# A constant matrix product in light steps, an allowance for transfers, an earlier input request and a dropped carry copy, in a scan kernel fused with an MLP

## The chip, the core and the metric

The kernel runs on one core of one Trainium2 chip. A core has five engines that each execute their own instruction queue in order: PE (TensorE, matrix products), DVE (VectorE), ACT (ScalarE), POOL (GpSimd) and SP (SyncE, which here only issues DMAs). All values are fp32. The metric is device time in microseconds of one execution, and the time before is a median of three runs.

## The reference

The input `x` is 8 images of 64 x 64 pixels with 96 channels. Two layers follow each other, each with a residual. The first normalises groups of channels, projects to 2 x 192 channels (`xc` and a gate `z`), filters `xc` with a 3 x 3 depthwise convolution and SiLU, and runs a selective scan over the 4096 pixels in four orders (`K = 4`: rows, columns, and both backwards) with 192 channels of 16 states:

```python
def step(h, inp):
    ul, dl, Bl, Cl = inp
    dA = jnp.exp(dl[..., None] * A)
    h = dA * h + (dl * ul)[..., None] * Bl[:, :, None, :]
    y = jnp.einsum('bkdn,bkn->bkd', h, Cl)
    return (h, y)
```

The four results are added, normalised, multiplied by the gate and projected back to 96 channels. The second layer normalises again, doubles the image's size in both directions by a Fourier filter, applies a matrix of 96 x 384, a quadratic polynomial and a matrix of 384 x 96, filters and samples down again, and adds the residual.

## The kernel before

**The scan steps.** One image has 4 orders (`k` = 1, 0, 2, 3) of 4 chunks of 1024 pixels, and each chunk has 24 tiles (`NT`) of 8 channels x 16 states = 128 partitions. That makes 16 chunks and 384 tiles per image, 3072 in all. The main loop makes one step per tile. The work of a tile is spread over the engines:

- `fetch` (L1004): SP issues a DMA that brings `dub`, 8 rows of `dl * u` each repeated over 16 partitions, 6 steps ahead. There are 4 buffers, so the DMA of tile i+6 waits until POOL has used that of tile i+2.
- `product_b` (L1012): POOL multiplies `dub` by B, 3 steps ahead.
- `decay` (L1016): PE spreads `dl` over the states into PSUM tile `pd` (2 products, 2 buffers), one step ahead, and ACT takes the exponential in place.
- `scan` (L1029): DVE runs the recurrence. `product_c` (L1038): DVE multiplies by C in two of three tiles; in the third (`by_pool`) POOL does, a step later. `hold` (L1042): a copy of the last state into column `g` of `carry`, on DVE, or on ACT for the `by_pool` tiles; the next chunk's scan of the same channels starts from it.
- `sums` (L1054): every second step PE adds states up into `py`, and `store` sends it to DRAM every 8 tiles.

Since `pd` has two buffers, `decay` of tile i+1 on PE waits until DVE is done with tile i-1.

**The input of a chunk.** `prepare` (L911) makes what the 24 tiles share: `begin` asks for `u` (two DMAs on SP, one buffer), `project` multiplies it on PE into `px`, and `delta` makes `dl` and `du` in three thirds. The main loop (L1151) asks for the next chunk's `u` in step 20 of 24; `project` stands first among the side work of step 0.

**The side work.** While the scan of image b runs, the rest of image b-1 (`tail`, L604, which normalises and gates the scan's result, then `mlp`, L737) and the start of image b+1 (`front`, L474, with `conv`, `lay` and `gate`) run as generators that a planner, `Side`, advances once per step. A generator yields what its next piece costs, in us per engine. A step gives each engine an allowance (`CAPS`, first number), which can be saved up to the second number; a piece that doesn't fit waits for a later step. Pieces also need one of three PSUM banks (`side.free`). DMAs cost nothing in this account: `load_x` issues one 192 KB transfer per step, `tail.begin` (loads `ye`) four per three steps, `tail.block` four at once (`ty`, `tz`), `lay` one per step. `advance` runs after `hold`, so on PE the side work of step i stands between `decay` of tile i+1 and `sums`, and all of it ahead of `decay` of tile i+2. In the last image `tail` starts within the fourth order, and its `mlp` runs after the last scan.

Of the kernel before, what the change touches and what calls it, by code (L numbers as in the profile page):

```python
# [23 lines left out]
NCH = L // T  # L24
MB = 512
NT = DI // 8
# [11 lines left out]
class Side:  # L38
# [7 lines left out]

    CAPS = dict(pe=(2.2, 2.9), act=(2.3, 3.0), dve=(1.5, 1.5), pool=(1.4, 2.7))

    def __init__(self, pool):
        self.pool = pool
        self.free, self.given = list(range(BANKS)), []
        self.urgent, self.hurried, self.later = [], [], []
        self.queue, self.active = [], []
        self.stores = []
        self.alone = {}
        self.begun = 0
        self.caps, self.left = None, {}

    def bank(self, name):
        n = self.free.pop(0)
# [9 lines left out]
    def emit(self, entry, spare):  # L72

        first = True
        while entry[1] is not None:
            need = dict(entry[1])
            banks, more = need.pop("bank", 0), need.pop("more", False)
            if need.pop("holds", False):
                spare = 0
            if not (first or more) or (banks and len(self.free) - spare < banks):  # L80
                return True
            if self.caps:
                if any(c > self.left[e] for e, c in need.items()):
                    return True
                for e, c in need.items():
                    self.left[e] -= c
            entry[1] = next(entry[0], None)
            first = False
        return False
# [15 lines left out]
    def advance(self, caps, more=1, spare=1, taken=0.0):  # L105

        self.caps = caps
        if caps:
            self.left = {e: min(self.left.get(e, 0.0) + c, most) for e, (c, most) in caps.items()}
            self.left["pe"] -= taken
        self.free += self.given
        self.given = []
        for active, spare_ in ((self.stores, 0), (self.hurried, 0), (self.active, spare)):
            for entry in list(active):
                if not self.emit(entry, spare_):
                    active.remove(entry)  # L120
            for _ in range(2):
                if self.urgent and active is self.hurried:
                    self.start(self.urgent, self.hurried, 0)
        for _ in range(more):
            if not self.queue or not self.start(self.queue, self.active, spare):
                break
# [7 lines left out]
def kernel(ctx: ExitStack, tc: tile.TileContext, a: dict, out: bass.AP):  # L134
    nc = tc.nc
    x = a["x"]
# [17 lines left out]
    ident = load("ident", [128, 128])  # L154
# [43 lines left out]
    sel_b = cp.tile([128, 8, NS, 8], F32, name="sel_b")  # L198
# [18 lines left out]
    with tc.tile_pool(name="ps0", bufs=1, space=PSUM) as ps0, tc.tile_pool(name="setup", bufs=1) as c0p:  # L217
# [55 lines left out]
        for j in (9, 7, 5, 3):  # L273
            c = (1.0 if j % 4 == 1 else -1.0) / math.factorial(j)
# [19 lines left out]
        for quarter in range(2):  # L294
            grid = wave[:, cols[SIDE, quarter]]
            start, stop = quarter == 0, quarter == 1
# [4 lines left out]
                start=start,  # L301
                stop=stop,
                skip_group_check=True,
            )
        for quarter in range(2):
            grid = wave[:, cols[SIDE, quarter]]
            start, stop = quarter == 0, quarter == 1
# [50 lines left out]
    side = Side(pss)  # L358
# [25 lines left out]
    bp = Room()  # L384
# [10 lines left out]
    def load_x(t, b):  # L395

        for w in range(0, 32, 8):
            for wh in range(2):
                w0 = 32 * wh + w
                nc.sync.dma_start(t[64 * wh : 64 * wh + 64, w : w + 8, :], x[b, :, w0 : w0 + 8, :])  # L400
                yield {}


    def pause(n):
# [69 lines left out]
    def front(b):  # L474
# [4 lines left out]
        v, got = {}, {}  # L479
# [10 lines left out]
            z_dram[b] = dr.tile([DI, L], F32, tag="z", name="z")  # L490

        def piece(g):
            yield {}
            t = bp.tile([128, 4, C], F32, tag="x", name="x", bufs=4)
            for wh in range(2):
                w0 = 32 * wh + 4 * g
                nc.sync.dma_start(t[64 * wh : 64 * wh + 64], x[b, :, w0 : w0 + 4, :])
            yield {}
            yield {}
            yield {}  # L500
            return t
# [55 lines left out]
        def lay(n):  # L557

            yield {}
            while not all((b, n, blk) in filtered for blk in range(8)):  # L560
                yield {}
            yield {}
            for h0 in range(0, H, 8):
                h1 = h0 + 8
                if n == 0:
                    src = v["xt"][0][:, h0:h1].rearrange("p h w -> p (h w)")
                    nc.sync.dma_start(u_dram[b][0][0:128, W * h0 : W * h1], src)
                else:
                    u = u_dram[b][0][128:192].rearrange("c (h w) -> c h w", h=H)
                    for p in range(2):  # L570
                        nc.sync.dma_start(u[:, h0:h1, 32 * p : 32 * p + 32], v["xt"][1][64 * p : 64 * p + 64, h0:h1])
                yield {}
            laid.add((b, n))

        def gate(n, g):
# [22 lines left out]
        parts, last = stats_items(piece, lambda: v["pad"], got)  # L598
        start = [bp.open("front"), (1, 1, begin), *parts, last, (4, 4, norm)]
# [4 lines left out]
    def tail(b, keep, pairs=True):  # L604

        v = {}

        def begin():
            yield {}
            keep["x1"] = bp.tile([128, 32, C], F32, tag="x", name="x", bufs=1, depth=0)  # L610
            while (b, "even") not in summed:
                yield {}
            v["ye"] = [bp.tile([C, H, W], F32, tag=f"ye{f}", name=f"ye{f}", bufs=1) for f in range(HF)]
            for h0 in range(0, H, 8):
                for f in range(HF):
                    nc.sync.dma_start(
                        v["ye"][f][:, h0 : h0 + 8].rearrange("p h w -> p (h w)"),
                        y_dram[b][0][f * C : f * C + C, W * h0 : W * h0 + 8 * W],
                    )
                    if f == 1 or h0 % 16:  # L620
                        yield {}
            yield {}
            yield {}

        def block(g):
# [5 lines left out]
            yz = [bp.tile([C, HF, 8, H], F32, tag=tag, name=tag, bufs=n) for tag, n in (("ty", 4), ("tz", 3))]  # L631
            for t, src in zip(yz, (y_dram[b][1], z_dram[b])):
                for f in range(HF):
                    nc.sync.dma_start(
                        t[:, f].rearrange("p w h -> p (w h)"), src[f * C : f * C + C, MB * g : MB * g + MB]
                    )
# [13 lines left out]
            for f in range(HF):  # L650
# [3 lines left out]
                t = two[f][1]  # L654
# [10 lines left out]
            n = two[0][0]  # L665
            t = side.again(n, "pn")
# [23 lines left out]
            halves = (0, 1) if pairs else (g // 4,)  # L690
            g %= 4
            rows = slice(64 * halves[0], 64 * halves[-1] + 64)
            for _ in range(3):
                yield {}
            for i0 in (0, 4):
                yield dict(bank=1, pe=1.7)
                n, t = side.bank("po")
# [3 lines left out]
                for i in range(4):  # L701
                    if i == 2:
                        yield dict(pe=0.87, act=0.5, more=True)
                    for f in range(HF):
                        for wh in halves:
# [4 lines left out]
                                start=False,  # L710
                                stop=(f == 1),
# [6 lines left out]
            if not v["left", g]:  # L718
                keep["done"].add(g)

        def piece(g):
            yield {}
            while g // 2 not in keep["done"]:
                yield {}
            return keep["x1"][:, 4 * g : 4 * g + 4, :]
# [3 lines left out]
        parts, keep["last"] = stats_items(piece, None, keep["got"])  # L729
        blocks += [parts[g] for g in (6, 7, 4, 5, 2, 3, 0, 1)]  # L730
        return (
            [bp.open("residual"), bp.open("tail"), (1, 1, begin), (4, 0, lambda: load_x(keep["x1"], b))]
            + blocks
            + [bp.close()]
        )

# [250 lines left out]
    tiles = []  # L987
    for b in range(images):
        for k in (1, 0, 2, 3):
            order = range(NCH) if k < 2 else range(NCH - 1, -1, -1)  # L990
            for n, c in enumerate(order):
                got = {}
                for i in range(NT):
                    q, n8 = divmod(i, 8)
                    s, j = n8 % 2, n8 // 2
                    tiles.append(
                        dict(b=b, k=k, i0=c * T, first=n == 0, i=i, q=q, s=s, j=j, g=8 * q + 4 * s + j, got=got)
                    )
                    tiles[-1]["by_pool"] = i % 3 == 2
    carry = pp.tile([128, NT], F32, tag="carry", name="carry", bufs=1)  # L1000

# [36 lines left out]
    def product_c(t):  # L1038
        t["hc"] = sp.tile([128, T], F32, tag="hc", name="hc", bufs=4)
        (nc.gpsimd if t["by_pool"] else nc.vector).tensor_tensor(t["hc"], t["h"], t["got"]["cr"], ALU.mult)  # L1040

    def hold(t):  # L1042
        end = T - 1 if t["k"] < 2 else 0
        (nc.scalar.copy if t["by_pool"] else nc.vector.tensor_copy)(  # L1044
            carry[:, t["g"] : t["g"] + 1], t["h"][:, end : end + 1]
        )
# [61 lines left out]
    with tc.manual_schedule():  # L1108
# [4 lines left out]
        n = len(tiles)  # L1113
# [8 lines left out]
        for i in range(n + 4):  # L1122
            t = tiles[i] if i < n else None
            at = i % (NT * NCH * K)
            if t and t["i"] == 0:
                b = t["b"]
# [21 lines left out]
                    side.queue += tail(b, keep, pairs=False)  # L1148
                    total = 0

            if i % NT == 20 and i + 4 + NT < n:  # L1151
                nxt = tiles[i + 4 + NT]
                begin, *side.later = prepare(nxt["b"], nxt["k"], nxt["i0"], nxt["got"])
                side.urgent.append(begin)
            if i % NT == 0:
# [12 lines left out]
            if t:  # L1168
# [9 lines left out]
                0 if 7 <= i % NT <= 21 else 1,  # L1178
                0.95 * (bool(ends) + bool(adds)),
            )  # L1180
            if ends:
                sums(tiles[i - 3 : i - 1])
                if tiles[i - 2]["j"] == 3:
                    side.stores.append([g := store(tiles[i - 2]), next(g)])
# [92 lines left out]
```

## Time and profile before

| | |
|---|---|
| median of 3 runs | 11395.91 us (11393.15 to 11407.87) |
| the profiled execution | 11378.34 us |
| its span in the profile | 11376.5 us |
| first scan starts, last scan starts | 143 us, 11099 us after the span's start |
| steps of the scan | 3072, 3.57 us each on average |
| mean granted TensorE clock | 0.929 of full speed |
| DMA | 2401 MB, mean 211 GB/s |

The page gives the busy time of each engine, then rows of tenths over 40 equal slices of the span. "PEclk" is the clock that TensorE was granted, in tenths of full speed. Groups of instructions follow as line, engine, operation, output<-inputs, shapes and count, then the total busy time, the mean duration in ns and the idle time of the engine just before such instructions. Windows give the busy time of each engine in a stretch and, after it, the granted clock, the DMA engines' share and the rate.

In the record of the granted clock there are only two values, full and half. There are 273 stretches at half clock, 1620 us together. 128 of them are 3.41 us long, 117 are 6.83 us, and all the others multiples of 3.41 us.

### The profile page before, as it was taken

What the parts mean: (1) busy time and instruction counts of PE and PEld (TensorE: products, weight loads), DVE (VectorE), ACT (ScalarE), POOL (GpSimd) and SP (SyncE); (2) the same over time, 40 slices, a digit from 0 to 9 for tenths busy, and PEclk for the clock granted to TensorE, in tenths of its full rate; (3) what the DMA queues carried; (4) which work ended last, traced back from release to release, by engine and by line L of the source; (5) the groups of instructions that cost most, each with busy time, mean ns of one, the idle gap of its engine ahead of it and who ended that gap; (6) DMA issues with size and microseconds to landing.
All of it is one profiled execution on the core that took longest, in us unless ns stands there. A gap on an engine that the chain in (4) does not pass through costs nothing. (4 is left out here: it accounts for less than half of the span.)

```text
span 11376.5 us, 134621 instructions
## 1 busy us (share of the span) xinstructions
PE 9587.4 (84%) x43368; PEld 3052.7 (27%) x43368; DVE 10255.8 (90%) x8223; ACT 5926.8 (52%) x8474; POOL 10186.7 (90%) x4665
## 2 busy tenths in 40 slices
PE   7687778989789887899788997898978988788878
PEld 2121112322123222332123321233212322123224
DVE  5999989999899999999989998999989999899980
ACT  4455444656456554555545555455644556455443
POOL 4999989999999999999999999999999999999980
PEclk9889889999899998999999998999989999899988
DMA  6878888899888898888988989889888899888871
GB/s 148 210 195 220 199 211 210 215 226 235 218 205 216 224 230 221 213 212 223 234 204 217 223 221 235 206 215 226 230 220 207 215 227 236 215 208 208 225 190 47
DMA packets 1045094, 2401.09 MB, mean 211 GB/s; under 512 B 293948, under 2 KB 315708, under 8 KB 1044392
## 3 DMA queue, kind: packets, MB, share of 16 engines
q1 hardware_dynamic: 1040872, 2391.03, 84.2%
q8 instruction: 349, 5.72, 0.2%
q14 instruction: 353, 2.89, 0.1%
q10 hardware_dynamic: 3520, 1.46, 0.1%
HBM read 1929.05 MB, written 328.73 MB: 198 GB/s over the span
## 5 line engine op out<-in xcount | busy, mean ns | idle before, releaser
L1014 POOL TENSOR_TENSOR bb<-dub,br 128x1024 f32<-128x1024 f32 x3072 | 7177.6, 2359 | 282.9 <-DMA dub<-du 171.9
L1027 ACT ACTIVATE pd<-pd,neg_a 128x1024 f32<-128x1024 f32 x3072 | 3341.1, 1088 | 4612.2 <-PE pd L1020 4366.3
L1020 PE MATMUL pd<-dl,sel_b 64*128 64x512 f32 x12288 | 3762.3, 685 | 1551.3 <-DVE carry L1044 1411.6
L1034 DVE TENSOR_TENSOR_SCAN pd<-pd,carry,bb 128x1024 f32<-128x1024 f32 x1536 | 3610.8, 2351 | 334.4 <-ACT carry L1044 208.9
L1040 POOL TENSOR_TENSOR hc<-h,cr 128x1024 f32<-128x1024 f32 x1024 | 2414.5, 2358 | 510.8 <-DVE h L1034 435.4
L1040 DVE TENSOR_TENSOR hc<-pd,cr 128x1024 f32<-128x1024 f32 x2048 | 2508.2, 1225 | 156.7 <-PE py L1063 14.9
L1020 PEld LDWEIGHTS pd<-dl,sel_b 64*128 64x128 f32 x12288 | 1036.0, 196 | 3944.1 <-issue 2678.0
L1063 PE MATMUL py<-hc,sel_r 128*32 128x512 f32 x12288 | 1825.0, 664 | 19.0 <-POOL hc L1040 13.9
L1034 DVE TENSOR_TENSOR_SCAN h<-pd,carry,bb 128x1024 f32<-128x1024 f32 x768 | 1796.6, 2339 | 16.2 <-ACT pd L1027 15.1
L1034 DVE TENSOR_TENSOR_SCAN pd<-pd,bb 128x1024 f32<-128x1024 f32 x512 | 1173.3, 2292 | 165.8 <-ACT carry L1044 119.9
L521 PE MATMUL pc<-pad,convr 96*128 96x512 f32 (+1 forms) x2304 | 862.7, 618 | 2.0 <-issue 2.0
L1034 DVE TENSOR_TENSOR_SCAN h<-pd,bb 128x1024 f32<-128x1024 f32 x256 | 583.5, 2279 | 22.9 <-ACT pd L1027 21.7
L977 POOL TENSOR_TENSOR u<-dl,u 128x512 f32<-128x512 f32 x384 | 486.4, 1273 | 127.2 <-DMA br<-xd 127.0
L1063 PEld LDWEIGHTS py<-hc,sel_r 128*32 128x32 f32 x12288 | 253.5, 112 | 1174.8 <-issue 904.5
L933 PE MATMUL px<-u,xp 64*64 64x512 f32 x1536 | 453.6, 647 | 107.0 <-DMA u<-u 107.0
L810 PEld LDWEIGHTS p<-w2q,mq 128*100 128x100 f32 x4800 | 452.6, 168 | 287.1 <-issue 221.4
L810 PE MATMUL p<-w2q,mq 128*100 128x96 f32 x4800 | 513.0, 258 | 5.1 <-ACT mq L804 5.1
L803 PE MATMUL ph<-xu,w 96*128 96x500 f32 x960 | 503.1, 629 | 9.4 <-ACT xu L797 4.8
L958 PE MATMUL pv<-xd,dt_w 64*64 64x512 f32 x1536 | 417.8, 634 | 9.2 <-ACT xd L943 9.0
L521 PEld LDWEIGHTS pc<-pad,convr 96*128 96x128 f32 (+1 forms) x2304 | 265.2, 163 | 562.6 <-issue 561.1
L804 ACT ACTIVATE mq<-ph,b 128x500 f32<-128x500 f32 x480 | 323.2, 679 | 77.4 <-PE ph L803 73.7
L1044 DVE COPY carry<-pd 128x1 f32<-128x1 f32 x2048 | 302.4, 148 | 0.0
(151 smaller groups left out, 6321.6 us busy)
## 6 DMA issues: line engine op xcount, KB each, us to landing
dub<-du SPq DMA_DIRECT2D x3072, 512.0 KB
u<-u SPq DMA_DIRECT2D x256, 384.0 KB
du<-u SPq DMA_DIRECT2D x768, 128.0 KB
y<-yq SPq DMA_DIRECT2D x768, 128.0 KB
br<-xd SPq DMA_DIRECT2D x256, 256.0 KB
cr<-xd SPq DMA_DIRECT2D x256, 256.0 KB
yp<-y SPq DMA_DIRECT2D x384, 128.0 KB
yp<-u SPq DMA_DIRECT2D x192, 128.0 KB
```

What stands on the lines that cost most here:

```text
L521: nc.tensor.matmul(t[rows].rearrange("p (i j) -> p i j", i=8), weights[:, cs], v["pad"][:, 8 * blk + kw : 8 * blk + kw + 8, kh : kh + H], ...
L803: nc.tensor.matmul(t[:, :px], w1[:, m, :], xu, start=True, stop=True)
L810: nc.tensor.matmul(t[:SIDE, C * i : C * i + C], sq[:, m, row], w2q[:, m, :], start=(m == 0), stop=(m == 2))
L933: nc.tensor.matmul(p[rows], xp[rows, k, q, :], v["u"][rows, q, :], start=(q == 0), stop=(q == 2), skip_group_check=True,)
L958: nc.tensor.matmul(t[rows], dt_w[rows, k, 64 * q : 64 * q + 64], v["xd"][rows], start=True, stop=True, skip_group_check=True,)
L977: nc.gpsimd.tensor_tensor(v["u"][:, q, :], got["dl"][:, q, :], v["u"][:, q, :], ALU.mult)
L1014: nc.gpsimd.tensor_tensor(t["bb"], t["dub"], t["got"]["br"], ALU.mult)
L1020: nc.tensor.matmul(pd[:, MB * hf : MB * hf + MB], sel_b[rows, 4 * t["s"] + t["j"]].rearrange("p n c -> p (n c)"), t["got"]["dl"][rows, t[" ...
L1027: nc.scalar.activation(pd, pd, AF.Exp, scale=neg_a[:, t["k"], t["g"] : t["g"] + 1])
L1034: nc.vector.tensor_tensor_scan(t["h"][:, ::step], pd[:, ::step], t["bb"][:, ::step], 0.0 if t["first"] else held, ALU.mult, ALU.add)
L1040: (nc.gpsimd if t["by_pool"] else nc.vector).tensor_tensor(t["hc"], t["h"], t["got"]["cr"], ALU.mult)
L1063: nc.tensor.matmul(py[r0 : r0 + 32], sel_r[:, t["j"], :], t["hc"][:, MB * hf : MB * hf + MB], start=(t["j"] == 0), stop=(t["j"] == 3 and t ...
```

## The change

Five things are edited; none alters what is computed.

1. `CAPS` gets a `dma` entry of 270 per step, saved up to 450, in KB. The generators that issue large transfers now yield `dma=200` (or 262 and 131 in `lay`) ahead of each, so that `load_x`, `front.piece`, `lay`, `tail.begin` and `tail.block` wait for the allowance, and `tail.block` issues one transfer per advance instead of four at once.
2. In `tail`, the load of the residual `x` stands behind the first two blocks instead of ahead of all.
3. `turn_over`, called in each step between `side.advance` and `sums`: where the planner has given out under 1.0 us of PE work in this step (`sums` counted) and a bank is free, PE multiplies `ident` by 512 columns of `sel_b`, both constants, into that bank. Nothing reads the result.
4. From step 48 on, the next chunk's `u` is asked for in step 16 instead of 20.
5. `hold` does nothing in the last chunk of an order.

```diff
-    CAPS = dict(pe=(2.2, 2.9), act=(2.3, 3.0), dve=(1.5, 1.5), pool=(1.4, 2.7))
+    CAPS = dict(pe=(2.2, 2.9), act=(2.3, 3.0), dve=(1.5, 1.5), pool=(1.4, 2.7), dma=(270, 450))
...
+                self.spent += need.get("pe", 0.0)
...
-        self.caps = caps
+        self.caps, self.spent = caps, taken
...
         for w in range(0, 32, 8):
             for wh in range(2):
                 w0 = 32 * wh + w
+                yield dict(dma=200)
                 nc.sync.dma_start(t[64 * wh : 64 * wh + 64, w : w + 8, :], x[b, :, w0 : w0 + 8, :])
-                yield {}
...
             for h0 in range(0, H, 8):
+                yield dict(dma=262 if n == 0 else 131)
...
                 for f in range(HF):
+                    yield dict(dma=200)
                     nc.sync.dma_start(
                         v["ye"][f][:, h0 : h0 + 8].rearrange("p h w -> p (h w)"),
...
                 for f in range(HF):
+                    yield dict(dma=200)
                     nc.sync.dma_start(
                         t[:, f].rearrange("p w h -> p (w h)"), src[f * C : f * C + C, MB * g : MB * g + MB]
...
-            [bp.open("residual"), bp.open("tail"), (1, 1, begin), (4, 0, lambda: load_x(keep["x1"], b))]
-            + blocks
+            [bp.open("residual"), bp.open("tail"), (1, 1, begin)]
+            + blocks[:2]
+            + [(4, 0, residual)]
+            + blocks[2:]
...
+    def turn_over():
+
+        if side.spent < 1.0 and side.free:
+            n, p = side.bank("idle")
+            nc.tensor.matmul(p, ident, sel_b[:, 0:4].rearrange("p j n c -> p (j n c)"), start=True, stop=True)
+            side.give(n)
+
     def hold(t):
+        if t["last"]:
+            return
...
-            if i % NT == 20 and i + 4 + NT < n:
-                nxt = tiles[i + 4 + NT]
+            ahead = 4 if i < 2 * NT else 8
+            if (i + ahead) % NT == 0 and i + ahead + NT < n:
+                nxt = tiles[i + ahead + NT]
...
+            turn_over()
             if ends:
                 sums(tiles[i - 3 : i - 1])
```

In the built program the change adds 827 products on PE and takes 512 copies off DVE and 256 off ACT. All other instructions are kept in number. The largest amount that SP is to issue between two `dub` loads falls from 2304 KB to 1920 KB at the start of an image and from 3264 KB to 1728 KB in the last image's end.

More of the change, by code (lines that the diff above doesn't have):

```diff
@@ L59, in __init__ @@
         self.caps, self.left = None, {}
+        self.spent = 0.0
     def bank(self, name):
@@ L492, in piece @@
         def piece(g):
-            yield {}
+            yield dict(dma=200)
             t = bp.tile([128, 4, C], F32, tag="x", name="x", bufs=4)
@@ L561, in lay @@
                 yield {}
-            yield {}
             for h0 in range(0, H, 8):
+                yield dict(dma=262 if n == 0 else 131)
                 h1 = h0 + 8
@@ L571, in lay @@
                         nc.sync.dma_start(u[:, h0:h1, 32 * p : 32 * p + 32], v["xt"][1][64 * p : 64 * p + 64, h0:h1])
-                yield {}
+            yield {}
             laid.add((b, n))
@@ L619, in begin @@
                     )
-                    if f == 1 or h0 % 16:
-                        yield {}
             yield {}
@@ L633, in block @@
                 for f in range(HF):
+                    yield dict(dma=200)
                     nc.sync.dma_start(
@@ L692, in block @@
             rows = slice(64 * halves[0], 64 * halves[-1] + 64)
+            while "x" not in v:
+                yield {}
             for _ in range(3):
@@ L719, in block, with residual @@
                 keep["done"].add(g)
+        def residual():
+            yield from load_x(keep["x1"], b)
+            v["x"] = True
         def piece(g):
@@ L998 @@
                     )
+                    tiles[-1]["last"] = n == NCH - 1
                     tiles[-1]["by_pool"] = i % 3 == 2
```

## The prediction

> **What bounds the kernel now.** I read the page's busy rows first, then windows by chunk, then the record of the granted clock, and last the timeline of one chunk that stalls.
>
> ```profile
> PE 9587.4 (84%) x43368; PEld 3052.7 (27%) x43368; DVE 10255.8 (90%) x8223; ACT 5926.8 (52%) x8474; POOL 10186.7 (90%) x4665
> PEclk9889889999899998999999998999989999899988
> ```
>
> DVE and POOL stand level at 90%, so neither alone is the bound, and a gain can come only out of the 10% in which both idle, some 1100 us. PE is busy for less and its clock is not always whole. How this spreads over chunks of 24 steps is in windows (stretch, us, then PE, PEld, DVE, ACT and POOL busy, clock, DMA share, GB/s):
>
> ```profile
> 1206.00:1292.00 86.00, 61.37 (x226) 14.13 (x222) 76.67 (x60) 34.31 (x46) 78.30 (x36) 0.80 0.80 197
> ...
> 1522.00:1612.00 90.00, 61.94 (x242) 14.43 (x234) 76.56 (x60) 37.31 (x52) 76.08 (x36) 0.88 0.97 226
> 1612.00:1712.00 100.00, 81.04 (x332) 22.65 (x334) 86.83 (x74) 44.68 (x67) 91.98 (x44) 0.87 0.84 205
> 1980.00:2060.00 80.00, 76.79 (x448) 32.94 (x440) 77.36 (x60) 47.80 (x69) 77.81 (x36) 1.00 0.88 217
> ```
>
> The last row is a chunk with much side work for PE and the clock at 1.00: 80 us, POOL busy for 77.8 of them. That is the floor. The first row has hardly any side work, the same DVE and POOL time, clock 0.80, and takes 86. The two middle rows are the start of an image, where the transfers of `tail` pile up. **So two things cost time: a slow PE in light chunks, and the pile-up once per image.**
>
> How the clock matters is seen in one step (timeline, chunk at 1292):
>
> ```profile
> 1338.75 0.15 DVE L1044 COPY carry<-pd 128x1 f32<-128x1 f32 x1
> 1338.82 2.34 DVE L1034 TENSOR_TENSOR_SCAN h<-pd,carry,bb 128x1024 f32<-128x1024 f32 x1
> ...
> 1339.04 1.13 PE L1020 MATMUL pd<-dl,sel_b 64*128 64x512 f32 x4 [1.46 <-DVE carry L1044]
> ...
> 1340.21 1.09 ACT L1027 ACTIVATE pd<-pd,neg_a 128x1024 f32<-128x1024 f32 x1 [2.50 <-PE pd L1020]
> ...
> 1341.40 2.36 DVE L1034 TENSOR_TENSOR_SCAN pd<-pd,carry,bb 128x1024 f32<-128x1024 f32 x1 [0.25 <-ACT carry L1044]
> ```
>
> The copy frees `pd`, PE spreads (1.13), ACT takes the exponential (1.09), and the next scan starts 2.50 us after the copy's end. Where the tile between is a `by_pool` one DVE has only its scan (2.34) to do meanwhile, so it waits 0.25 us even at full clock. At half clock `decay` takes 2.06 (1341.21 in the same view) and the wait grows by 0.93, or more if half-clock `sums` (1.93 instead of 1.06) stand ahead of it on PE.
>
> **The change, part by part.**
>
> *The constant product.* The clock changes at multiples of 3.41 us. These are such windows, one after another (PE busy is the second number after the stretch):
>
> ```profile
> 1313.95:1317.37 3.42, 1.60 (x12) 0.49 (x12) 3.31 (x4) 0.84 (x2) 3.42 (x3) 1.00 0.98 280
> 1317.37:1320.78 3.41, 1.66 (x12) 0.33 (x4) 3.38 (x4) 0.91 (x2) 3.41 (x2) 1.00 0.65 155
> 1320.78:1324.20 3.42, 2.67 (x8) 0.70 (x12) 3.14 (x3) 1.43 (x3) 3.42 (x3) 0.50 0.88 240
> 1324.20:1327.61 3.41, 3.33 (x12) 0.54 (x4) 3.41 (x3) 0.60 (x1) 3.41 (x2) 0.50 0.30 71
> 1327.61:1331.03 3.42, 1.84 (x13) 0.49 (x12) 3.32 (x4) 1.75 (x2) 3.30 (x2) 1.00 0.90 228
> ...
> 1337.85:1341.27 3.42, 1.19 (x6) 0.39 (x6) 3.31 (x3) 1.06 (x2) 2.82 (x2) 1.00 0.97 285
> 1341.27:1344.68 3.41, 3.41 (x12) 0.62 (x12) 3.24 (x2) 1.22 (x3) 3.38 (x2) 0.50 1.04 235
> ```
>
> After 1.66 and after 1.19 the clock is halved; after 3.33 it is whole again. Over the whole trace, 258 of the 273 half-clock stretches follow a window in which PE was busy for less than half; of the 2577 full-clock windows that don't end so, 24 were. All but a few stretches end after a window over 90% busy. The Trainium skill says it otherwise ("TensorE: Matmul & The Clock Gate", What's actually happening): half clock comes after a window in which PE is idle. By that rule only the 12 stretches whose window was under a tenth busy would be of this kind, 12 x 5.9 us, and 827 products would be nearly pure cost, since PE works in each step anyway. By the trace the line lies near half, and I go by the trace.
>
> A light step has `decay` (1.13) and, every second time, `sums` (1.06): 1.13 and 2.19 us of 3.57. One 512-column product of 128 rows takes 1.12 alone (the `ident` product in `sums`, same timeline); a second one in a row adds 0.86 (two of `conv` take 1.99 at 2704.18, one 1.13). I take 0.87. 625 of the 827 stand in steps without other side work. They make 2.0 and 3.1 of 3.57, both above half. I laid 0.87 us per product into PE's gap of its step in the trace of before: 157 of the 273 windows pass half, and these precede 819 of the 1620 half-clock us. The other windows are stalls, where no product is emitted or PE is held.
>
> What a half-clock us costs: six light chunks of image 0 take 84.0 us at 28.2 us half clock each; chunks at full clock take 80.3. That is 0.13. A fit over triples of steps gives 0.09 to 0.26 by the kind of chunk. I take 0.14: 819 x 0.14 = **-115 us** (ends 0 and 1555 x 0.14 = -218, all of it within the scan).
>
> Against it: PE runs in order, and behind the product wait `sums` and the next `decay`. In the same laying, 444 products fit whole into the gap, the others lack 264 us in sum. Also, 389 carry a wait for the bank's last reader on DVE, ACT or PE; most were done a step before. The tight `decay` is the one that follows a step with 3.5 us of DVE work, and 1.13 + 1.06 + 1.06 = 3.25, start to start, fits. I take a tenth of the lack, **+20** (ends 0 and +264).
>
> *Allowance, later residual, earlier request.* In the first image start:
>
> ```profile
> 1609.17 2.34 POOL L1014 TENSOR_TENSOR bb<-dub,br 128x1024 f32<-128x1024 f32 x1 [4.97 <-DMA dub<-du]
> 1610.00 2.62 SPq L922 DMA_DIRECT2D u<-u  x2
> 1611.54 2.36 DVE L1034 TENSOR_TENSOR_SCAN pd<-pd,carry,bb 128x1024 f32<-128x1024 f32 x1 [5.67 <-POOL bb L1014]
> ...
> 1619.39 1.96 PE L933 MATMUL px<-u,xp 64*64 64x512 f32 x2 [12.04 <-DMA u<-u]
> ...
> 1628.84 0.75 DVE L678 SCALAR_TENSOR_TENSOR ps<-ty,ln_g,pn 96x512 f32<-96x512 f32 x1 [8.37 <-ACT pn L672]
> ```
>
> `dub` comes late behind `ye`, `x`, `ty` and `tz`, so DVE stands 5.67 us; `u` is issued late on SP, PE waits 12.04 for it with all behind it, and DVE stands 8.37 and, between, 1.51 more: 15.5 us. The wait for `u` recurs in images 1 to 7 and nowhere else in the steady loop: 12.0, 9.3, 4.3, 10.3, 12.3, 8.6, 11.4, 68.2 in sum. Four more steps are 14 us, more than each. On SP the two requests move ahead of four `dub` issues (1.3 us each pair; SP mostly waits for `bb`); the buffer of `u` is free, since its last `du` goes out before step 9. Side transfers in the image's first chunk fall from 459 to 323 KB a step and rise from 267 to 339 in the second; with 512 for `dub` that asks some 235 GB/s, and a chunk has run at 262. So the late `dub` should shrink, not vanish. Scaling 15.5 by 9.7/12.0 gives 12.6 per image, 88 for seven; I keep 75 of it, since some load moves into the next chunk: **-75** (ends -110 and +20). `tail`'s POOL and DVE work also moves later, over chunks with more of DVE's and less of POOL's; that evens itself out. `lay` in smaller doses moves a few gates one chunk on: **-5**.
>
> *No last copy.* 512 copies of 0.15 on DVE, of which the next scan sees about 0.06 (start 1338.75, scan 1338.82): 31 us; `decay` of the tile after next starts as much earlier. POOL at the floor hides a third. ACT's 256 have slack. **-20** (ends 0 and -76).
>
> Sum: -115 + 20 - 75 - 5 - 20 = -195. Against the profiled 11378 that makes 11183; the median of before lies 17.6 higher, so for the median 11396 - 195 = **11201 us**.
>
> **Rivals.**
> - *The clock is nearly whole* (0.17): -218 + 20 - 88 - 5 - 30 = -321, 11075. For it: light chunks hold much of the half clock. Against: stalls of `tail` remain, where few products go.
> - *Only transfers and copies pay* (0.13): what the clock gives is taken by later `decay` and by POOL at its floor, -80 to -100, 11305.
> - *The products stand in the way* (0.08): each in PE's queue ahead of `decay`, the missing 264 us reach DVE and, by the skill's rule, the clock gives nothing: +264 - 100 = +164, 11560. It decides from 215/827 = 0.26 us per product on. For it: the 389 waits, which may end late, and that a half-clock step with a product has 2.06 + 1.74 + 1.93 = 5.7 us of PE work, over its 3.57; against: the 1.46 us for which PE waits ahead of the quoted `decay`, a wait that totals 1411.6.
> - *The pile-up only moves* to the second chunk and clock gains are small (0.04): no change, 11390.
>
> **Numbers.** Likeliest 0.58. The range reaches to the first two rivals, 11080 to 11325. 0.2% is 23 us, what a measurement here can tell from no change: faster 0.88, within 0.04, slower 0.08.
>
> **What would show it.** Mean clock 0.96 to 0.97, and under 130 half-clock stretches; light chunks near 81; the wait of `px` for `u` gone from images 1 to 7, first two chunks of an image 187 to about 177; POOL's wait for `dub` (171.9) under 120. I am wrong if the clock stays at 0.93, or if PE's idle time before `decay` ends mostly on PE itself, by the constant product, with DVE's waits for `pd` grown.

## The result and the profile after

The changed kernel takes 11231.7 us (median of 4 runs, 11211.0 to 11240.0) beside 11400.4 for the kernel before on the same chip: a ratio of 0.9849 (95% interval 0.9831 to 0.9866), or 169 us less. The profiled execution has a span of 11225.8 us. Below, "us by ratio" is a ratio's difference times 11400: runs stood on several chips, each beside the kernel before on the same chip, so ratios are compared and not times.

The busy rows and the clock of the page after:

```profile
PE 10052.8 (90%) x45022; PEld 3217.9 (29%) x45022; DVE 10212.6 (91%) x7711; ACT 5906.0 (53%) x8218; POOL 10175.5 (91%) x4665
PEclk9999999999999999999999999999999999999998
```

PE is busy for 465 us more and DVE and POOL do nearly what they did, in 151 us less. The clock's row has lost its eights but for the last slice; the mean is 0.974 instead of 0.929, and 91 half-clock stretches with 582 us are left of 273 with 1620. The 151 us are 170 us less from the first scan to the last and 20 us more after the last scan, to which the last section comes back.

Windows of the same chunks as before (stretch, us, then PE, PEld, DVE, ACT and POOL busy, clock, DMA share, GB/s), first the light one of image 0, then the first two of the next image, its fifth and its sixth:

```profile
1171.00:1250.00 79.00, 67.07 (x262) 17.29 (x260) 75.59 (x59) 33.85 (x45) 77.25 (x36) 1.00 0.86 213
1476.00:1557.00 81.00, 69.53 (x266) 17.65 (x268) 76.10 (x60) 34.39 (x46) 73.22 (x34) 0.98 0.97 230
1557.00:1648.00 91.00, 77.98 (x338) 21.87 (x330) 82.62 (x67) 42.87 (x62) 90.73 (x45) 1.00 0.98 245
1830.00:1920.00 90.00, 74.68 (x339) 22.75 (x336) 77.32 (x63) 42.30 (x65) 78.04 (x38) 0.91 0.77 202
1920.00:2000.00 80.00, 75.33 (x426) 30.67 (x418) 77.37 (x60) 48.07 (x69) 77.50 (x36) 1.00 0.88 214
```

The light chunk is at its floor: 79 us, POOL busy for 77 of them. The pile-up chunks fell from 90 and 100 to 81 and 91, and in the second POOL is now busy throughout (90.73 of 91). The full-clock chunk is unchanged. But the fifth chunk takes 90, where the kernel before took 87:

```profile
1893.00:1980.00 87.00, 68.76 (x284) 19.55 (x280) 77.85 (x63) 45.44 (x70) 79.23 (x38) 0.90 0.84 216
```

Neither POOL (78.04) nor DVE (77.32) has more to do there than before, so something new stands still. **This loss inside the gain is what most of the experiments turn on.**

How the product sits in a light chunk, in the timeline of PE after:

```profile
1211.02 1.13 PE L1032 MATMUL pd<-dl,sel_b 64*128 64x512 f32 x4 [0.83 <-DVE carry L1065]
1212.08 1.12 PE L1058 MATMUL idle<-sel_b,ident 128*128 128x512 f32 x2
1214.62 1.13 PE L1032 MATMUL pd<-dl,sel_b 64*128 64x512 f32 x4 [1.41 <-DVE carry L1065]
```

The product takes 1.12 us of a gap, and the next `decay` still waits 1.41 us for DVE after it: nothing is held up.

Three waits of the kernel after (us in total, times, longest):

```profile
POOL bb L1026 <- DMA dub<-du: 167.9, 111, 6.7
ACT t1s L769 <- DMA t<-t1s: 95.2, 24, 9.2
PE px L944 <- DMA u<-u: 35.0, 2, 24.3
```

The same three of the kernel before:

```profile
POOL bb L1014 <- DMA dub<-du: 171.9, 148, 6.8
ACT t1s L758 <- DMA t<-t1s: 58.9, 25, 5.1
PE px L933 <- DMA u<-u: 107.0, 16, 24.3
```

PE's wait for `u` is gone but for the two at the kernel's start. POOL's wait for `dub` is nearly what it was. And ACT waits 95.2 us ahead of its copies into `t1s` for stores out of `t1s`, instead of 58.9. `t1s` belongs to `up_h` in `mlp`: ACT copies two PSUM banks into one of its two buffers, and two DMAs store that to DRAM.

### The profile page after: what moved, and what is told of

It reads as the page before. It is cut to its first block, busy times and chain, and to the rows that moved or that the text cites. A ratio compares the mean times of both kernels' runs of the same rounds, so it can differ in the third digit from the quotient of the medians.

```text
span 11225.8 us, 137177 instructions
## 1 busy us (share of the span) xinstructions
PE 10052.8 (90%) x45022; PEld 3217.9 (29%) x45022; DVE 10212.6 (91%) x7711; ACT 5906.0 (53%) x8218; POOL 10175.5 (91%) x4665
## 5 line engine op out<-in xcount | busy, mean ns | idle before, releaser
L1026 POOL TENSOR_TENSOR bb<-dub,br 128x1024 f32<-128x1024 f32 x3072 | 7174.5, 2359 | 254.7 <-DMA dub<-du 167.9
L1032 PE MATMUL pd<-dl,sel_b 64*128 64x512 f32 x12288 | 3528.3, 647 | 942.1 <-DVE carry L1065 625.6
L1032 PEld LDWEIGHTS pd<-dl,sel_b 64*128 64x128 f32 x12288 | 967.7, 186 | 3230.9 <-issue 1534.8
L1084 PE MATMUL py<-hc,sel_r 128*32 128x512 f32 x12288 | 1723.2, 620 | 34.6 <-POOL hc L1052 34.4
L1058 PE MATMUL idle<-sel_b,ident 128*128 128x512 f32 x1654 | 949.4, 656 | 5.2 <-DVE ty L682 5.2
L944 PE MATMUL px<-u,xp 64*64 64x512 f32 x1536 | 427.4, 630 | 37.4 <-DMA u<-u 35.0
L1058 PEld LDWEIGHTS idle<-sel_b,ident 128*128 128x128 f32 x1654 | 252.9, 191 | 613.5 <-issue 575.5
```

The source lines that it names most:

```text
L944: nc.tensor.matmul(p[rows], xp[rows, k, q, :], v["u"][rows, q, :], start=(q == 0), stop=(q == 2), skip_group_check=True,)
L1026: nc.gpsimd.tensor_tensor(t["bb"], t["dub"], t["got"]["br"], ALU.mult)
L1032: nc.tensor.matmul(pd[:, MB * hf : MB * hf + MB], sel_b[rows, 4 * t["s"] + t["j"]].rearrange("p n c -> p (n c)"), t["got"]["dl"][rows, t[" ...
L1058: nc.tensor.matmul(p, ident, sel_b[:, 0:4].rearrange("p j n c -> p (j n c)"), start=True, stop=True)
L1084: nc.tensor.matmul(py[r0 : r0 + 32], sel_r[:, t["j"], :], t["hc"][:, MB * hf : MB * hf + MB], start=(t["j"] == 0), stop=(t["j"] == 3 and t ...
```

## The experiments

### What the constant product is worth

**no_product**, the change without it:

```diff
-            turn_over()
```

> The changed kernel without the constant products, all else kept. Theory (the clock carries more than half of the gain, 95 us of 169): near 11325 us, mean clock back to 0.93 to 0.94, image 0, where no transfers of a tail run, back from 1334 to about 1375 us. Rival (transfers and the earlier request carry it, the products only fill idle time): within 25 us of 11231.

Measured: 11309.6 us, ratio 0.9913 (0.9898 to 0.9927), clock 0.930, 269 half-clock stretches. The product is worth 0.0064, 73 us by ratio. In the profiles the first image goes back from 1334 to 1380 us.

**product_only**, the kernel before with the product and nothing else (848 of them in its trace).

> The kernel before with nothing but the constant products added. Theory (the clock's gain does not rest on the transfers: 99 us in the scan steps and 20 lost after the last scan, as between no_product and the changed kernel): 11310 to 11340, clock 0.965 to 0.972, image 0 near 1335 us. Rival 1 (the two gains overlap, since stalls by transfers halve the clock too, so the product alone is worth more): 11280 to 11305. Rival 2 (it pays only where transfers do not stall): 11345 to 11375.

Measured: 11327.8 us, ratio 0.9935 (0.9922 to 0.9947), clock 0.972, image 0 at 1340 us. That is 74 us by ratio, as from the other side, so the clock's gain and that of the other edits add up; an overlap isn't seen within the intervals.

**short_product**, 64 columns instead of 512 at the same 827 places of the loop:

```diff
-            nc.tensor.matmul(p, ident, sel_b[:, 0:4].rearrange("p j n c -> p (j n c)"), start=True, stop=True)
+            nc.tensor.matmul(p[:, :64], ident, sel_b[:, 0:1].rearrange("p j n c -> p (j n c)")[:, :64], start=True, stop=True)
```

> The changed kernel with products of 64 columns instead of 512, at the same places. Theory (what counts is that PE is busy for half of a 3.4 us window, and 64 columns add only some 0.1 to 0.3 us): clock 0.93 to 0.945, 11285 to 11310, near the kernel without products. Rival (a window without any product is what halves the clock): clock 0.97 and 11231 or less, since the short products hold up nothing.

Measured: 11316.6 us, ratio 0.9912 (0.9897 to 0.9927). Span and clock of the changed kernel, of no_product and of short_product, in this order:

```profile
core 0: 11225.8 us, clock 0.974
core 0: 11304.4 us, clock 0.930
core 0: 11329.5 us, clock 0.936
```

The places are the same, the columns an eighth (387 us busy in sum instead of 949), and both clock and time are near those without products. So in this kernel it isn't whether PE works in a window that counts but for how much of it, and the prediction's choice of the trace's line near half over the Trainium skill's idle window ("TensorE: Matmul & The Clock Gate", What's actually happening) holds.

**product_less** and **product_more** move the bound, to 393 and 1236 products in their traces instead of 827.

```diff
-        if side.spent < 1.0 and side.free:
+        if side.spent < 0.9 and side.free:
...
-        if side.spent < 1.0 and side.free:
+        if side.spent < 1.9 and side.free:
```

> The changed kernel with the bound for a product at 0.9 us, so that only steps without sums and without any side work for PE get one: 393 of 826. Theory (a light step with sums has 2.19 us of PE work of 3.57 and stays over half without a product; only the even ones need it): clock 0.965 to 0.975 and 11205 to 11235, with the waits of decay behind a product down from 98 us. Rival (windows straddle steps, and half of the products keeps half of the clock): clock near 0.95, 11250 to 11280.

> The changed kernel with the bound for a product at 1.9 us of PE work in the step instead of 1.0, which makes 1235 products of 826. Theory (the steps with 1.0 to 1.9 us of work are over half busy already, so these products only stand in the way of the next decay): clock within 0.01 of 0.974, 11240 to 11280. Rival (half-clock stretches are left in such steps): clock 0.985, 11200 to 11225.

Measured: product_less 11251.4 us, ratio 0.9873 (0.9856 to 0.9890), clock 0.959, 171 stretches: near the rival. So products in light steps with `sums` keep the clock up too. The likely reason is that the 3.41 us windows don't keep to the steps: 158 of the 171 stretches again follow a window in which PE was busy for less than half.

product_more 11441.1 us, ratio 1.0031 (1.0021 to 1.0040), slower than the kernel before, and the theory was far too low: 409 products more cost 0.0182, 207 us by ratio, half a us each, at a clock of 0.978. A window of product_more in the 13th chunk of the second image, where `conv` runs:

```profile
2536.00:2626.00 90.00, 90.00 (x349) 24.26 (x348) 79.26 (x63) 47.94 (x65) 78.38 (x36) 1.00 0.77 198
```

and the same chunk of the changed kernel:

```profile
2492.00:2574.00 82.00, 81.66 (x332) 21.53 (x324) 78.81 (x64) 47.99 (x65) 78.39 (x36) 1.00 0.86 216
```

PE has no gap in this chunk even without them (81.66 of 82). Ten products instead of one make it 8 us longer: here a product costs nearly all of its length (nine more, 0.86 us each behind another), in the light step shown above nothing. The bound of 1.0 stands between the two.

### What the transfers and the earlier request are worth

**no_allowance** issues the transfers as before (the diff's `dma` yields, the `dma` entry and the residual's new place undone), **late_request** asks for `u` in step 20 throughout:

```diff
-            ahead = 4 if i < 2 * NT else 8
+            ahead = 4
```

> The changed kernel with the transfers issued as before (no dma allowance, residual ahead of the blocks), but with products, earlier request and without the last copies. Theory (the allowance itself is worth what is left of 75 us once the earlier request has taken the wait for u away): 11255 to 11290 us, the loss in the first two chunks of an image. Rival 1 (the allowance only moves the work, since chunks 4 and 5 of an image became longer by 3 and 4 us): 11210 to 11240. Rival 2 (it carries all of the 75): 11300.

> The changed kernel with u asked for in step 20 of 24 throughout. Theory (with the transfers spread out, u comes in time in most images also 4 steps ahead): 11231 to 11260 us, with some waits of px for u of a few us in images 1 to 7. Rival (the request is what removed the stall): near 11300, with seven waits of 5 to 12 us.

Measured: no_allowance 11277.5 us, ratio 0.9889 (0.9871 to 0.9906), so the allowance is worth 46 us by ratio. Its first two chunks of images 1 to 6 take 91.2 and 97.1 us on average instead of 81.7 and 92.1, its fourth and fifth 86.0 and 87.1 instead of 90.6 and 90.9: the allowance wins 14.5 us at the start and gives 8.4 back later.

late_request 11186.0 us, ratio 0.9804 (0.9784 to 0.9824): **neither theory; the kernel is 51 us by ratio faster without the earlier request.** No wait of `px` for `u` over 2 us is left after image 0 either, so the allowance alone had removed it. Without the request the allowance with the copies is worth 0.9935 (product_only) - 0.9804 = 0.0131, 149 us.

Most of what the request costs is seen in the timeline of the changed kernel, in the fifth chunk of image 1, where the request of step 16 goes out:

```profile
1887.53 1.27 SPq L933 DMA_DIRECT2D u<-u  x2
...
1889.89 0.94 SPq L775 DMA_DIRECT2D t<-t1s  x2
...
1892.68 1.60 SPq L775 DMA_DIRECT2D t<-t1s  x2
...
1901.30 0.59 ACT L769 COPY t1s<-p 100x512 f32<-100x512 f32 x1 [7.32 <-DMA t<-t1s]
1901.79 1.09 ACT L1039 ACTIVATE pd<-pd,neg_a 128x1024 f32<-128x1024 f32 x1
...
1902.98 2.30 DVE L1046 TENSOR_TENSOR_SCAN pd<-pd,bb 128x1024 f32<-128x1024 f32 x1 [5.44 <-ACT pd L1039]
```

768 KB of `u` (two DMAs of 384) go out just ahead of the stores of `t1s`. ACT needs a buffer of `t1s` back and waits 7.32 us for a store to land; the exponential of `decay` stands behind that copy in ACT's queue, and DVE waits 5.44 for it.

**request_only**, the kernel before with the earlier request alone.

> The kernel before with nothing but u asked for in step 16 instead of 20 from step 48 on. Theory (without the allowance the wait for u is real, 68 us over seven images, but the earlier load also stands ahead of the stores of t1s): waits of px for u gone after image 0, 20 to 50 us gained, 11355 to 11385. Rival 1 (the collision costs as much as with the allowance, 45 us, and the stall is due to late dub anyway): 11400 to 11450. Rival 2 (no collision here): 11320 to 11345.

Measured: 11405.1 us, ratio 1.0006 (0.9995 to 1.0017): no change. Two of its waits:

```profile
POOL bb L1014 <- DMA dub<-du: 222.6, 149, 6.9
PE px L933 <- DMA u<-u: 34.8, 2, 24.0
```

PE's 68 us in images 1 to 7 are gone as asked, and POOL waits 222.6 us for `dub` instead of 171.9. In images 1 to 6 the second chunk, where PE's wait stood, goes from 100.2 us only to 98.4 on average, and the first, in which the request goes out, grows from 87.0 to 90.8. The DMA engines are busy for 0.98 of that first chunk in both kernels, so it is likely that whoever is served earlier there makes another late. The total of POOL's wait alone doesn't show it: product_only, which leaves the request where it was, has 211.7.

One difference stays open. product_only and no_allowance differ only by the request and the copies, and there the two gain 0.0046, 52 us by ratio. The copies alone could not be told from nothing (below), and request_only gains nothing. So with the product and without the allowance the request seems to pay; why was not tried.

**t1s_3** gives `t1s` a third buffer, **t1s_3_late** takes the late request besides:

```diff
-            s = bp.tile([SIDE, 2, MB], F32, tag="t1s", name="t1s")
+            s = bp.tile([SIDE, 2, MB], F32, tag="t1s", name="t1s", bufs=3)
```

> The changed kernel with three buffers of t1s instead of two. Theory (the earlier load of u stands ahead of the stores of t1s on SP and in the DMA engines, ACT waits 95 us for these stores to free a buffer, and the exponentials wait behind it): the wait shrinks to under 30 us, the fifth chunk of an image falls from 91 to about 85 us, the whole to 11180 to 11200. Rival (the fifth chunk is long for the tail's work that was moved into it): 11225 to 11240.

> As t1s_3, and u asked for in step 20 of 24 throughout. Theory (the two remedies work on the same wait and only overlap in part, 56 us of it are left with the late request): 11145 to 11175. Rival (the late request has taken all that there was): 11180 to 11195.

Measured: t1s_3 11203.9 us, ratio 0.9816 (0.9802 to 0.9829), a little short of the theory. t1s_3_late 11159.1 us, ratio **0.9780 (0.9766 to 0.9793)**, as the theory had it. ACT's wait for the stores is 49.9 us in t1s_3; in late_request and then in t1s_3_late (us, times):

```profile
  DMA t<-t1s: 55.7, 25
  DMA t<-t1s: 15.4, 11
```

The fifth chunk of images 1 to 6 goes from 90.9 us to 86.0, 85.1 and 81.6. Its windows in late_request and in t1s_3_late:

```profile
1826.00:1910.00 84.00, 71.05 (x338) 22.17 (x340) 77.49 (x64) 42.49 (x64) 78.24 (x38) 0.96 0.79 210
```

```profile
1826.00:1907.00 81.00, 69.33 (x344) 22.12 (x344) 77.44 (x63) 42.84 (x65) 78.20 (x38) 1.00 0.81 208
```

With the same work on DVE, ACT and POOL, the chunk comes down to its floor and to a clock of 1.00. So ACT's wait for these stores is the cause of that chunk's loss. About 40 us of late_request's gain fall into the fifth chunks, 12 into the first (79.6 us instead of 81.7); the other chunks cancel nearly. In the first chunks of images 1 to 7 POOL waits 2.3 us for `dub` instead of 6.5, so there, too, the earlier request seems to have made another transfer late.

**product_less_best**, t1s_3_late with the bound of 0.9:

> t1s_3_late (three buffers of t1s, late request; 11159 us) with the bound for a product at 0.9 us. Theory: 11130 to 11165. Rival: 11180 to 11210.

Measured: 11187.3 us, ratio 0.9813 (0.9795 to 0.9831), 38 us by ratio worse than with 1.0. The fastest version tried is t1s_3_late.

### What the copies are worth

**copy_always**:

```diff
-        if t["last"]:
-            return
```

> The changed kernel with the last state copied in every chunk. Theory: 768 more copies cost 15 to 30 us, so 11246 to 11260, spread evenly over the fourth chunk of every order. Rival (hidden, since POOL stands at its floor): within 10 us of 11231.

Measured: 11247.6 us, ratio 0.9853 (0.9836 to 0.9870) against 0.9849 (0.9831 to 0.9866). The intervals lie over each other almost wholly. The median is 16 us higher, by ratio it is 5 us: a small gain and none can't be told apart.

## Why the prediction was right, and where not

The forecast was -195 us and the result is -169. The clock's part works as put: the mean clock (0.974) is a little above the 0.96 to 0.97 named, and 91 stretches are under the 130. That the sum of the transfers' part comes out is luck, as shown below.

- **The constant product**: forecast -115 + 20 = -95, measured -73 and -74. The count was too careful (157 stretches were to go, 178 went between no_product and the changed kernel), the price per half-clock us too high, and the two errors cancel in part. In this pair of profiles 993 us of half clock go and the scan steps become 99 us shorter, 0.10 for each, where the forecast had 95 for 819, 0.12; from the kernel before to product_only it is 0.07. In image 0, whose light chunks had given 0.13, the price holds: 46 us for about 320. In images 1 to 6 it is only some 7 us for about 94 per image, perhaps since there the half clock lies in chunks that something else holds up anyway; that was not tried. After the last scan, where the forecast put nothing, 20 us are lost in this pair. The +20 for products in the way isn't visible as such; half a us for each product that product_more adds shows that a looser bound would have cost far more.
- **Allowance and request**: forecast -75 together. The change without product gains 99 us by ratio with the copies, forecast at -100 with `lay`, so the sum fits. Its inner working doesn't, so this is luck. The step that failed is "Four more steps are 14 us, more than each. On SP the two requests move ahead of four `dub` issues (1.3 us each pair; SP mostly waits for `bb`)". It priced the moved request by its time on SP and by the buffer of `u`. It left out the bytes: what is served behind them in the DMA engines, and who waits for that. In the changed kernel that was mostly ACT behind the stores of `t1s`, about 40 of 51 us; in the kernel before all of the gain went, likely to POOL behind `dub`. The allowance was undervalued: without the request it is worth 149 us with the copies, beside it only 46. The sum came out as 149 less 51.
- **POOL's wait for `dub`** was to fall under 120 and stayed at 167.9. That sign was wrong, though the first two chunks came to 174 us, even below the 177 named. The wait fell where the forecast looked, in the first three chunks of images 1 to 7 (12.9 us per image before, 7.2 after), and grew in the eleventh (from 5.3 to 9.6), which takes 86 us in both kernels.
- **Copies**: -20 forecast, not resolved.
- **The slower rival**, products ahead of `decay`, was the right mechanism for product_more, whose loss it describes; at the change's bound it doesn't decide. The rule by which it let the clock give nothing fell with short_product.

## What to carry to other kernels

Where a clock follows how busy an engine is, as here, a filler pays in steps that have a gap and costs its whole length in steps that have none, so bound it by the work already in the step, and measure the length that the clock needs rather than whether there is work at all. A load that is asked for earlier is not free just because its buffer is: list what is in the DMA queue behind it in the new place and which engine stands waiting for that, above all an engine that has other work queued behind the wait. When a moved transfer removes a wait, look for the same time in another wait before counting it.

## What I had not expected of the hardware

After the last scan the kernel runs the last image's MLP, 277 to 278 us in the profiles of the kernel before and of no_product, and 292 to 300 us in those of the others, request_only among them, which has no products at all. The last 57 us of no_product and of the changed kernel:

```profile
11247.00:11304.40 57.40, 34.43 (x181) 21.08 (x180) 0.00 (x0) 12.45 (x20) 0.00 (x0) 0.83 0.27 75
```

```profile
11168.40:11225.80 57.40, 44.14 (x140) 25.42 (x136) 0.00 (x0) 9.23 (x15) 0.00 (x0) 0.50 0.22 60
```

After a gap the clock is halved in both. In the first it comes back, in the second PE stays at half clock to the end, though it is busy for 44 of 57 us. In the trace of before, 264 of the 273 half-clock stretches end with a window over 90% busy, while 258 began after one under half; a window at half clock with 2.67 of 3.42 us busy (at 1320.78 in the windows that the prediction shows) is followed by another at half clock. So half clock can keep itself up where PE has short pauses: the way back asks for more than the way down. Why the one execution got its full window and the other not was not tried, and one profile per kernel can't say how often each happens.
